# A graph-attention layer on one core: all q rows from gathered rows of h, and the ring of k|v rows used for the opening's loads

## The chip, the cores and the metric

The kernel runs on one core of one Trainium2 chip. The metric is device time in microseconds (us). Before the change the median of three runs is 1938.27 us (1937.52 to 1938.92). The profile shown here is of one execution with a span of 1932.2 us.

A core has five engines with queues of their own: TensorE (PE; PEld is its weight load), VectorE (DVE), ScalarE (ACT), GpSimd (POOL) and SyncE (SP, which only issues transfers here). Products of PE go to PSUM, in buffers that another engine has to read out before they are used again.

## The reference

There are 4096 nodes with 512 features. `adj` is a 4096x4096 matrix of 0 and 1, symmetric, with about 0.4% of ones and a full diagonal. One layer is computed:

```python
hs = layer_norm(x, ln1_scale, ln1_bias)            # sources
ht = layer_norm(h_target, ln1_scale, ln1_bias)     # targets
q = (ht @ Wq + bq).reshape(T, 8, 64) / 8
k = (hs @ Wk + bk).reshape(S, 8, 64)
v = (hs @ Wv + bv).reshape(S, 8, 64)
logits = where(adj != 0, einsum('thd,shd->hts', q, k), -1e30)
ctx = einsum('hts,shd->thd', softmax(logits), v)
ht = layer_norm(ht + ctx @ Wo + bo, ln2_scale, ln2_bias)
out = layernorm(x + ht + gelu(ht @ W1) @ W2)
```

W1 is 512x2048 and W2 is 2048x512. All numbers are float32.

## The kernel before

The kernel doesn't compute the dense logits. A target has some 17 neighbours on average, so it lists the neighbours of each target and gathers their k and v.

**k|v rows.** `project` takes x in 16 groups of 256 rows. `norm` loads a group, takes its moments and scales it; `turn` transposes it on PE and adds scale and bias on the way out of PSUM (L868); `source` multiplies it by Wk and Wv (L878), copies both products on ACT into one row of 1024 numbers (L880) and writes it to the table `kvd` in DRAM.

**Neighbour lists.** `edges` handles a tile of 128 targets. Its adjacency comes in four quarters of 128x1024, loaded into two buffers named `a` (L680). ACT takes the Sign of a quarter and counts its ones (L695), DVE numbers the ones and picks them with a maximum of eight (L699 to L725). `sort` orders the targets of one half (part A: the first 16 tiles, part B: the others) by their number of neighbours, and scatters their records (neighbour list, own index, moments of h) to DRAM, so that each sorted tile of 128 targets has a small cap on its list.

**q rows.** For the 16 tiles of part A, `front` gathers the rows of `h_target` that a sorted tile needs, scales them by the moments in the record, transposes them and multiplies them by Wq (L954 to L969). For part B, `target` computes q of all rows in their original order after the k|v rows (L889 to L900), writes q and the normalized row to a table `tqd`, and `front` only gathers from this table. In `finish` the normalized row is then added to the attention output, for part A with four transposes on PE into the same PSUM buffer (L1043), for part B with an add on DVE (L1056).

**Attention.** A ring of 17 slots of 128x1024 takes gathered k|v rows (L924, on POOL), one neighbour per slot, up to three slots at a time (`S`). DVE multiplies k by q (L1150) and sums by head (L1154), ACT takes Exp (L1158), DVE weights the v of two slots (L1103), ACT that of the third (L1123), and PE adds them up by transposing them into one PSUM buffer (L1111). For part B DVE first adds two slots (L1107). Gathers run four such steps ahead (`AHEAD`). A slot is free again when PE has read it. `finish` divides by the sums, multiplies by Wo (L1048) and applies the second layer norm.

**Feed-forward.** `feed` takes one group of two tiles (one tile for the first and the last group), multiplies by W1 (L1258), applies Gelu (L1261), multiplies by W2 (L1267), and `end` adds x, normalizes and scatters the rows to the output. W1 and W2 are loaded in four quarters by `load_quarter`.

**Order.** `_weave` merges several Python generators into one program by a running sum of costs that each yields; a planner may still move instructions within an engine's queue. Each engine then executes its queue in order. There are two weaves. The first holds `projections` (k|v rows, then part B's q rows), `prepare` (part A's lists and sort), `fill` (three more tiles of lists at double cost) and `begin` (the first three tiles of attention). The second holds attention, feed-forward, and the remaining lists with part B's sort.

Of the kernel before, what the change touches and what calls it, by code (L numbers as in the profile page):

```python
# [17 lines left out]
P = 128  # L18
# [425 lines left out]
def adj_resnorm_kernel(  # L444
# [66 lines left out]

    tqd = dram.tile([NBT * P, 2 * D], F32, name="tqd")
# [19 lines left out]
    with tc.tile_pool(name="keep", bufs=1) as keep:  # L532
# [17 lines left out]
        with ExitStack() as late:  # L550
# [5 lines left out]
            kvw = src.enter_context(tc.tile_pool(name="kvw", bufs=1))  # L556
            mid = ExitStack()
# [5 lines left out]
            first_x = ip.tile([P, G, D], F32, name="xin", bufs=3)  # L563
# [48 lines left out]
            def late_constants():  # L612
# [9 lines left out]
                                               ap=[[0, P], [1, D]]))  # L622
                pb = psi.tile([P, D], F32, name="pq", bufs=3)
# [49 lines left out]
            held, moms, hnorm = [], list(range(NT)), []  # L673
            mvh = wp.tile([P, NT, 2], F32, name="mvh")

            adjs = []

            def quarter(i, h):
                a = lp.tile([P, QW], I32, name="a", bufs=2)
                nc.sync.dma_start(a, adj[i * P:(i + 1) * P, h * QW:(h + 1) * QW])  # L680
                return a

            def edges(i):
# [4 lines left out]
                for h in range(NQ):  # L688
# [7 lines left out]
                    if n + 2 < NT * NQ:  # L696
                        adjs.append(quarter(*divmod(n + 2, NQ)))
# [59 lines left out]

            def moments(i):

                t = ip.tile([P, D], F32, name="hst", bufs=1)  # L760
                nc.sync.dma_start(t, h_target[i * P:(i + 1) * P, :])
                stats(ip, t, mvh[:, i, :], "n0")
# [60 lines left out]
            def project(order, t=None):  # L823


                state = {}

                def scaled(t, rs, nm):
                    nc.scalar.activation(t, t, AF.Identity, bias=nm, scale=rs)

                def norm(n, t=None):
                    if n >= len(order):
                        return
                    kind, g = order[n]
                    if t is None:
                        t = ip.tile([P, G, D], F32, name="xin", bufs=3)
                        nc.sync.dma_start(t, rows(x if kind == "x" else h_target, g))
                    if kind == "h":
                        rs, nm = hnorm[0]
                        for j in range(G):  # L840
                            i = g * G + j
                            scaled(t[:, j, :], rs[:, i:i + 1], nm[:, i:i + 1])
                        state[n] = t
                        return
                    mv = ip.tile([P, G, 2], F32, name="mv")
                    for j in range(G):
                        stats(ip, t[:, j, :], mv[:, j, :], "n1")
                    rs, nm = rstd_of(ip, mv, G, "n1")
                    for j in range(G):
                        scaled(t[:, j, :], rs[:, j:j + 1], nm[:, j:j + 1])  # L850
                    state[n] = t

                def turn(n):
# [3 lines left out]
                    bias = b1c if order[n][0] == "x" else b1r  # L857
                    hT = ip.tile([P, KC, GR], F32, name="hT")
                    for k2 in range(KC // 2):
# [6 lines left out]
                        for k in range(2):  # L866
                            kc = k2 * 2 + k
                            nc.scalar.activation(hT[:, kc, :], pt[:, k, :], AF.Identity,  # L868
                                                 bias=bias[:, kc:kc + 1], scale=s1c[:, kc:kc + 1])
                    state[n] = t, hT  # L870

                def source(n, j):
                    g, hT = order[n][1], state[n][1]
                    kvr = ip.tile([P, 2 * D], F32, name="row")
# [10 lines left out]
                def target(n, j):  # L885
                    g, hT = order[n][1], state[n][1]
                    pq = psi.tile([P, D], F32, name="pq", bufs=3)
                    for kc in range(KC):
                        nc.tensor.matmul(pq, hT[:, kc, j * P:(j + 1) * P], wq[:, kc, :],  # L889
                                         start=kc == 0, stop=kc == KC - 1)  # L890
                    pr = psi.tile([P, D], F32, name="pq", bufs=3)
                    for kc in range(KC):
                        nc.tensor.transpose(pr[:, kc * P:(kc + 1) * P],
                                            hT[:, kc, j * P:(j + 1) * P], ident)
                    tq = ip.tile([P, 2 * D], F32, name="row")
                    nc.vector.scalar_tensor_tensor(tq[:, :D], pq, HD ** -0.5, bqr,
                                                   op0=ALU.mult, op1=ALU.add)
                    nc.scalar.copy(tq[:, D:], pr)
                    r0 = (g * G + j - NA) * P
                    nc.sync.dma_start(tqd[r0:r0 + P, :], tq)  # L900
                    return 4.8

                with tc.manual_schedule(engines={mybir.EngineType.DVE}):
                    norm(0, t)
                    turn(0)
                    norm(1)
                yield 0.0
                for n, (kind, _) in enumerate(order):
                    while n + 2 < len(order) and order[n + 2][0] == "h" and not hnorm:
                        yield None  # L910
                    for j in range(G):
                        cost = (source if kind == "x" else target)(n, j)
                        if j == 0:
                            turn(n + 1)
                        else:
                            norm(n + 2)
# [24 lines left out]
            def front(i):  # L941
# [4 lines left out]
                if TILES[i][0] >= NA * P:  # L946
                    gather(tq, tqd, rec[:, ROW:ROW + 1])
                    tqs[i] = tq
                    return
# [27 lines left out]
            ring = kp.tile([P, RING, 2 * D], F32, name="kv")  # L977
# [31 lines left out]
            def finish(i, p, cps, group, hs, mv):  # L1009
# [3 lines left out]
                has = sp.tile([P, MAXE], BF16, name="has", bufs=1)  # L1013
                nc.vector.tensor_scalar(has[:, :cap], rec[:, E0:E0 + cap], 0.0, None, op0=ALU.is_gt)
                pm = sp.tile([P, MAXE, H], F32, name="pm", bufs=1)
                nc.vector.tensor_mul(pm[:, :cap, :], p[:, :cap, :],
                                     has[:, :cap].unsqueeze(2).to_broadcast([P, cap, H]))
# [21 lines left out]
                first = TILES[i][0] < NA * P  # L1039
                if first:  # L1040

                    for c in range(KC):
                        nc.tensor.matmul(pa[:, c * P:(c + 1) * P],  # L1043
                                         tq[:, D + c * P:D + (c + 1) * P], ident,
                                         is_transpose=True, start=c == 0, stop=False,
                                         skip_group_check=True)
                for c in range(KC):
                    nc.tensor.matmul(pa, ct[:, c, :], wo[:, c, :], start=c == 0 and not first,  # L1048
# [3 lines left out]
                if first:  # L1052
                    nc.scalar.copy(h, pa)
                    yield
                else:
                    nc.vector.tensor_add(h, pa, tq[:, D:])  # L1056
# [27 lines left out]

            def attention():
# [4 lines left out]
                def advance():  # L1090
                    for i in list(fronts):
                        step(fronts, i)
# [32 lines left out]
                for i in range(EARLY):  # L1125
                    prefetch(i)
                for i in range(EARLY):
                    fronts[i] = front(i)
# [303 lines left out]
```

## Time and profile before

| | PE | DVE | ACT | POOL |
|---|---|---|---|---|
| busy us | 1719.6 | 1443.7 | 1227.2 | 889.6 |
| share of the span | 89% | 75% | 64% | 46% |
| instructions | 7030 | 2637 | 3097 | 804 |

The transfers move 480 MB at a mean of 248 GB/s. Most of it is the gathers of k|v rows.

The page also cuts the span in 40 slices of 48 us. A digit is the busy share of a slice in tenths (9 is 90% or more); PEclk is the clock that was granted to TensorE in tenths of full speed, DMA the mean busy share of the 16 DMA engines:

```profile
PE   7978877788888889989999999899898989989996
...
DVE  5776764678797887757778789899897897878500
...
PEclk9989988889999899989999999999999999999998
DMA  9888867979878666567686888888878877776200
```

The first ten slices hold the opening (lists, k|v rows, part B's q rows, the first three tiles of attention), the last two or three the feed-forward that is left when attention is done. A busy digit of PE is not yet a rate: at a low clock the same work is busy for longer.

### The profile page before, as it was taken

How to read it: one execution, taken by the hardware profiler on the slowest of the kernel's cores; microseconds unless marked ns; L12 is line 12 of the kernel's file. 1: busy time of each engine (PE TensorE's matmuls, PEld its weight loads, DVE VectorE, ACT ScalarE, POOL GpSimd, SP SyncE). 2: the span in 40 equal slices, each digit the busy share in tenths (PEclk: the TensorE clock that was granted, in tenths of full speed). 3: DMA queues.
4: the chain of work that ended last, by engine and by line, in shares of the span. 5: the costliest groups of instructions: out<-in, count | busy, mean ns of one | idle time of the engine just before them, and what ended most of it. 6: DMA issues, size and time to landing. Idle time of an engine off the chain costs nothing. (4 is left out here: it accounts for less than half of the span.)

```text
span 1932.2 us, 23024 instructions
## 1 busy us (share of the span) xinstructions
PE 1719.6 (89%) x7030; PEld 1106.5 (57%) x7030; DVE 1443.7 (75%) x2637; ACT 1227.2 (64%) x3097; POOL 889.6 (46%) x804
## 2 busy tenths in 40 slices
PE   7978877788888889989999999899898989989996
PEld 3433333455566556657776666666565666656664
DVE  5776764678797887757778789899897897878500
ACT  5555654654786776657767677678686876666511
POOL 1000032524254445665575666777666655564201
PEclk9989988889999899989999999999999999999998
DMA  9888867979878666567686888888878877776200
GB/s 320 274 275 265 255 229 247 367 276 338 301 274 298 213 252 231 184 195 260 224 303 234 296 270 285 295 273 312 266 253 281 273 250 247 240 260 221 68 8 24
DMA packets 153262, 480.07 MB, mean 248 GB/s; under 512 B 24852, under 2 KB 29544, under 8 KB 153128
## 3 DMA queue, kind: packets, MB, share of 16 engines
q0 software_dynamic: 96720, 346.39, 52.3%
q1 hardware_dynamic: 48592, 109.03, 17.1%
q10 hardware_dynamic: 7816, 23.08, 3.0%
q8 instruction: 58, 0.95, 0.2%
q14 instruction: 76, 0.62, 0.1%
HBM read 439.15 MB, written 39.28 MB: 248 GB/s over the span
## 5 line engine op out<-in xcount | busy, mean ns | idle before, releaser
L924 POOL DMA_INDIRECT kv<-kvd,rec x603 | 697.4, 1157 | 495.1 <-PE cps L1111 201.0
L1267 PE MATMUL po<-w,gt 128*128 128x512 f32 x1024 | 476.2, 605 | 7.5 <-ACT gt L1261 4.0
L1258 PE MATMUL pf<-h2T,w 128*128 128x256 f32 (+1 forms) x2176 | 473.0, 370 | 5.3 <-DMA w<-in_L_gnn_W_dram 5.2
L1150 DVE TENSOR_TENSOR kv<-kv,tq 128x1536 f32<-128x1536 f32 (+2 forms) x211 | 352.2, 1676 | 135.5 <-DMA kv<-kvd,rec 108.5
L1258 PEld LDWEIGHTS pf<-h2T,w 128*128 128x128 f32 x2176 | 391.0, 192 | 75.3 <-issue 32.0
L1123 ACT ACTIVATE kv<-kv,pa 128x64 f32<-128x64 f32 x1520 | 390.4, 336 | 4.0
L1154 DVE TENSOR_REDUCE lg<-kv 128x24 f32<-128x1536 f32 (+2 forms) x211 | 350.2, 1666 | 1.6
L1267 PEld LDWEIGHTS po<-w,gt 128*128 128x128 f32 x1024 | 189.2, 195 | 192.8 <-issue 186.5
L1111 PEld LDWEIGHTS cps<-ident,kv 128*128 128x128 f32 x2008 | 237.8, 144 | 93.8 <-issue 47.2
L1111 PE MATMUL cps<-ident,kv 128*128 128x128 f32 x2008 | 263.1, 278 | 24.7 <-DVE kv L1107 17.5
L1103 DVE TENSOR_TENSOR kv<-kv,p 128x1024 f32<-128x1024 f32 (+1 forms) x211 | 249.5, 1188 | 25.7 <-ACT p L1158 24.4
L695 ACT ACTIVATE sg<-a 128x1024 uint8<-128x1024 int32 x128 | 135.0, 1056 | 161.1 <-DMA a<-in_adj_dram 126.0
L659 POOL TENSOR_TENSOR n_rs<-n_ve,mhalf 128x2 f32<-128x2 f32 (+2 forms) x51 | 46.9, 919 | 385.4 <-DVE n_ve L652 185.8
L878 PE MATMUL pq<-wv,hT 128*128 128x512 f32 x256 | 122.9, 624 | 20.1 <-ACT row L880 20.1
L1261 ACT ACTIVATE gt<-pf 128x512 f32<-128x512 f32 x128 | 76.4, 597 | 100.3 <-PE pf L1258 81.8
L878 PE MATMUL pq<-wk,hT 128*128 128x512 f32 x256 | 123.5, 625 | 17.0 <-ACT tq L954 10.5
L1261 ACT ACT_TABLE_LOAD x106 | 136.0, 1283 | 2.9 <-issue 1.2
L1048 PE MATMUL t<-wo,rb 128*128 128x512 f32 x256 | 126.3, 639 | 3.3 <-DVE rb L1035 3.3
L701 DVE MAX8 cand<-sg 128x8 uint16<-128x103 uint16 (+1 forms) x640 | 128.4, 251 | 0.7
L1158 ACT ACTIVATE p<-lg 128x24 f32<-128x24 f32 (+2 forms) x179 | 33.8, 189 | 130.5 <-DVE lg L1154 100.0
L878 PEld LDWEIGHTS pq<-wv,hT 128*128 128x128 f32 x256 | 50.0, 200 | 88.3 <-issue 57.0
L1158 ACT ACT_TABLE_LOAD x69 | 88.5, 1283 | 10.1 <-DVE lg L1154 9.0
(164 smaller groups left out, 1602.4 us busy)
## 6 DMA issues: line engine op xcount, KB each, us to landing
a<-in_adj_dram SPq DMA_DIRECT2D x128, 512.0 KB
kvd<-row ACTq DMA_DIRECT2D x32, 512.0 KB
kv<-kvd,rec POOLq DMA_INDIRECT x603
hst<-in_L_gnn_h_target_dram SPq DMA_DIRECT2D x32, 256.0 KB
tqd<-row SPq DMA_DIRECT2D x16, 512.0 KB
xin<-in_x_dram SPq DMA_DIRECT2D x15, 512.0 KB
rest_d<-gid SPq DMA_DIRECT2D x32, 160.0 KB
xin<-in_L_gnn_h_target_dram SPq DMA_DIRECT2D x8, 512.0 KB
```

Source lines behind the costliest of these rows:

```text
L695: nc.scalar.activation(sg, a, AF.Sign, accum_out=dpart[:, i, h:h + 1])
L701: nc.vector.max(cand[:, h * SQ + s, :], wd[:, w0:w1])
L878: nc.tensor.matmul(pkv, hT[:, kc, j * P:(j + 1) * P], w[:, kc, :], start=kc == 0, stop=kc == KC - 1)
L924: nc.gpsimd.indirect_dma_start(out=dst, out_offset=None, in_=table[:, :], in_offset=bass.IndirectOffsetOnAxis(ap=idx, axis=0))
L1103: nc.vector.tensor_tensor(v4, v4, p[:, j0:j0 + m, :].unsqueeze(3) .to_broadcast([P, m, H, HD]), ALU.mult)
L1111: nc.tensor.matmul(cps[:, c, :], kv[:, j, D + c * P:D + (c + 1) * P], ident, is_transpose=True, start=j0 + j == 0 and c == 0, stop=j0 + n ...
L1123: nc.scalar.mul(v, v, pa[:, hd:hd + 1])
L1150: nc.vector.tensor_tensor(kv[:, :n, :D], kv[:, :n, :D], tq[:, :D].unsqueeze(1).to_broadcast([P, n, D]), ALU.mult)
L1154: nc.vector.tensor_reduce(lg[:, :n, :], kv[:, :n, :D].rearrange("p j (h d) -> p j h d", h=H), AX.X, ALU.add)
L1258: nc.tensor.matmul(pf[:, k, :], w1[(f0 + k) // KC][:, kc, (f0 + k) % KC * P:((f0 + k) % KC + 1) * P], h2T[:, kc, :w], start=kc == 0, stop= ...
L1261: nc.scalar.activation(gt, pf, AF.Gelu_apprx_tanh)
L1267: nc.tensor.matmul(po[j], gt[:, k, j * P:(j + 1) * P], w2[(f0 + k) // KC][:, (f0 + k) % KC, :], start=False, stop=f0 + k == FC - 1, skip_g ...
```

## The change

The change does four things.

- All 32 sorted tiles get their q row from gathered rows of h in `front`. `target`, the table `tqd`, the second pass of h through `project` and the DVE add at the end of `finish` go.
- The ring of k|v slots exists from the start, and before the first gather its space takes the loads of the opening: 8 slots for adjacency quarters (`DEEP`), 4 slots for eight rows of h tiles, 5 slots for groups of x. So loads are asked for further ahead. `norm` is split in `request` (load, four groups ahead), `measure` (moments, three ahead) and `scale` (two ahead). The small buffers `hT` and `row` of the projection use the space of later buffers (`h2T`, `tq`).
- The first two quarters of W1 and W2 are loaded during the k|v rows, after the ninth and the eleventh group; the others at the start of the second weave. Wo and Wq are loaded later than before, at the fifth group.
- The weaves are set anew: the first holds the k|v rows, part A's lists, sort and first two fronts, and five more tiles of lists (`FILL`) at their plain cost. All of attention is in the second, and starts together with feed-forward.

Besides, the mask of filled list places in `finish` is fused with its multiplication into one instruction.

What it is for: to save the write and second read of part B's rows, to keep engines of the opening from waiting for transfers, and to let the opening be shorter.

```diff
+            ring = kp.tile([P, RING, 2 * D], F32, name="kv")
+            def xrows(n):
+                return ring[:, 12 + n % 5, :].rearrange("p (j d) -> p j d", j=G)
...
             def quarter(i, h):
-                a = lp.tile([P, QW], I32, name="a", bufs=2)
+                if i < NA + FILL:
+                    a = ring[:, (i * NQ + h) % DEEP, :].bitcast(I32)
+                else:
+                    a = lp.tile([P, QW], I32, name="a", bufs=2)
                 nc.sync.dma_start(a, adj[i * P:(i + 1) * P, h * QW:(h + 1) * QW])
...
-                    if n + 2 < NT * NQ:
-                        adjs.append(quarter(*divmod(n + 2, NQ)))
+                    ahead = min(n + DEEP - 1, n + 3 + n // 2)
+                    while len(adjs) < min(max(n + 3, min(ahead, (NA + FILL) * NQ)), NT * NQ):
+                        adjs.append(quarter(*divmod(len(adjs), NQ)))
...
+            def hrow(i):
+                return ring[:, DEEP + i // 2 % 4, i % 2 * D:(i % 2 + 1) * D]
             def moments(i):
-                t = ip.tile([P, D], F32, name="hst", bufs=1)
-                nc.sync.dma_start(t, h_target[i * P:(i + 1) * P, :])
+                while asked and len(asked) > NT - 4 - i:
+                    ask(asked.pop(0))
+                t = hrow(i)
...
-                tq = sp.tile([P, 2 * D], F32, name="tq", bufs=3)
-                if TILES[i][0] >= NA * P:
-                    gather(tq, tqd, rec[:, ROW:ROW + 1])
-                    tqs[i] = tq
-                    return
...
-                        cost = (source if kind == "x" else target)(n, j)
+                        cost = source(n, j)
                         if j == 0:
+                            request(n + 4)
+                            measure(n + 3)
                             turn(n + 1)
                         else:
-                            norm(n + 2)
+                            scale(n + 2)
...
-                if first:
-                    nc.scalar.copy(h, pa)
-                    yield
-                else:
-                    nc.vector.tensor_add(h, pa, tq[:, D:])
+                nc.scalar.copy(h, pa)
+                yield
...
-                for cost in _take(ed, 3 * steps):
-                    yield 2.0 * cost
+                for cost in _take(ed, FILL * steps):
+                    yield cost
...
-            _weave((projections(), 0), (prepare(), 0), (fill(), 0), (begin(), 0))
+            _weave((projections(), 0), (prepare(), 0), (fill(), 0))
...
-            t0 = UNIT / 2 * 3
-            _weave((att, t0 + PAUSE), (chain(feed(g) for g in range(len(GROUPS))), UNIT / 2 + LEAD),
-                   (other_lists(), t0 - 30.0))
+            _weave((att, 0), (chain(feed(g) for g in range(len(GROUPS))), 0), (other_lists(), WAIT),
+                   (weights(), 0))
```

## The prediction

> **What bounds the kernel now.** I read the table of stretches first, because the page's shares (PE 89%, DVE 75%) average four stages with different limits. The stages are cut where a line first or last appears: the k|v matmuls L878 end at 324 us, the feed-forward L1258 starts at 460, the last attention multiply L1150 is at 1801. Columns: stretch, its length, busy time and count of PE, PEld, DVE, ACT, POOL, then granted clock, DMA share, GB/s.
>
> ```profile
> 0.00:324.00 324.00, 264.11 (x680) 120.20 (x681) 218.82 (x903) 181.40 (x331) 42.59 (x58) 0.94 0.80 264
> 324.00:460.00 136.00, 108.46 (x401) 63.26 (x399) 91.42 (x189) 75.72 (x202) 46.25 (x43) 0.89 0.87 316
> ...
> 850.00:1000.00 150.00, 149.47 (x710) 106.11 (x709) 115.91 (x117) 106.59 (x296) 89.56 (x83) 1.00 0.77 260
> 1000.00:1815.00 815.00, 758.32 (x3291) 519.80 (x3290) 703.11 (x799) 581.49 (x1574) 512.41 (x440) 0.97 0.77 260
> ```
>
> From 850 to 1000 PE never pauses. From 1000 on PE (93%) and DVE (86%) hold each other: DVE waits for gathered rows, these for a free ring slot, the slot for PE. Before 460 nothing is full, so that is where time can be won. What stands there is in the waits of 0 to 324 us (engine, line, waited for: total us, times, longest):
>
> ```profile
> PEld pq L878 <- issue: 103.8, 404, 0.6
> ACT sg L695 <- DMA a<-in_adj_dram: 77.3, 42, 6.0
> DVE n_st L669 <- DMA hst<-in_L_gnn_h_target_dram: 32.0, 9, 6.4
> PEld pq L878 <- ACT row L880: 31.8, 20, 5.7
> ...
> PE pq L878 <- ACT row L880: 20.4, 11, 4.8
> ```
>
> ACT's Sign waits 77 us for adjacency, since only two quarters are in flight; the copy L880 that empties PSUM stands behind it, and PE waits 20 us for that copy. The timeline of DVE shows how attention opens (start, length):
>
> ```profile
> 348.07 1.76 DVE L1150 TENSOR_TENSOR kv<-kv,tq 128x1536 f32<-128x1536 f32 x1 [9.38 <-DMA kv<-kvd,rec]
> ```
>
> The first attention multiply is at 348, the first feed-forward matmul at 460. In these 112 us only 13 of 211 multiplies run.
>
> **The Trainium skill.** "DMA: Bandwidth & Descriptors", "Issuing engines are not separate DMA queues": transfers from SyncE, ScalarE and GpSimd interleave on the same 16 DMA engines. The trace agrees: with three issuers the rate is 264 GB/s at a share of 0.80, so a full share would be 264/0.80 = 330. "TensorE: Matmul & The Clock Gate", "Architectural detail: the array is 16× 32×32, not 1× 128×128": ACT and DVE are strict FIFO; hence the copy behind the Sign, as above. Same page, "Part 1: The HAM clock gate": the array falls back to half rate when idle and returns after sustained work. It fits: after a pause of 7.12 us at 352.8 four L893 transposes take 1.12 us, elsewhere 0.60. An idle opening costs twice.
>
> **The change, part by part.**
>
> *Loads in the opening.* Adjacency gets 8 ring slots in place of 2 buffers, x 5 in place of 3, h 4 rows of slots in place of 1. Nothing is computed less. The statistics of x run three groups ahead and Wo, Wq come later. I look for a new end of the opening as the largest of three floors.
> - PE: 8 records of 128x512 start 3.44 us apart (287.89 to 291.33), 0.43 each. A row tile has 16 of them, 6.9 us, and four transposes of 0.11 each: 7.3 us. 32 tiles take 234. With 7 for bias constants (8 matmuls of two records), 8 for two early q rows and the first start at 17: 266 us.
> - DVE: 219 us busy by 324, with 19 edge tiles scanned (154 Sign records at two each = 77 quarters). In the new order of instructions 23 tiles stand ahead of the first attention multiply. An edge tile is 9.8 us by its groups (L701 128, L699 52, L720 46, the rest 88, over 32), about 8.5 after overlap: 219 + 4 x 8.5 = 253, from a start near 19: 272.
> - DMA: 85.6 MB went by 324. Four adjacency tiles of 2.1 MB and two weight quarters (4.2 MB) are added, the early h reloads drop (about 1.5): 97 MB with the tiles loaded for the gap after it; some 90 before the last k|v row. At 330 GB/s: 273 us.
>
> Three streams near 270 us don't overlap perfectly; I take 90% of full for the fullest: about 300 us to the last k|v row. Bounds: 280 (97%) and 320 (nothing gained beyond the Wo/Wq reordering).
>
> *From there to attention.* Before, 24 us pass from the last L878 (324) to the first multiply (348), with 2 MB of weights loading at the same moment. After, these weights come earlier (at the 9th and 11th group); the last row still has to land and three gathers of about 1.2 us to be issued and land. I take 12 us: 312, a gain of 36. Bounds 292 and 332.
>
> *The 112 us to the first feed-forward matmul.* All 16 target groups' work goes: 128 L889 records (0.43), 64 L893 and 64 of the L864 transposes (0.11), 55 + 14 = 69 us of PE; also 8 h reloads, 16 writes and 16 gathers of 4 KB rows. In the new order attention has run 25 slots (about 9 multiplies) before the first feed-forward matmul, with one edge tile among it. Each takes 1.75 + 1.74 + 1.21 = 4.7 us on DVE, 5.2 with finish work: 47 + 10 for edges and waits = 57; I take 60. DVE sets this pace, PE has some 25 us to do and idles. Bounds 50 and 75. Gain 52. But two multiplies less are done by then than before (about 11): + 8 us.
>
> *q of the later 16 tiles on the way.* Each front gains four transposes, 8 records for q, and four transposes to add the row to the Wo result: 0.44 + 3.4 + 0.44 = 4.3 us of PE, 69 in all, in the stretch where PE is at 93%. ACT gains a scaling (0.81), four PSUM reads (0.46 each) and a copy (0.57), 3.2 us a tile, 51 in all; it is at 71% there. DVE exchanges the add L1056 (0.68) for the q scaling L969 (0.69). New waits: ACT's scaling waits for the h gather; the Exp and the third slot's products queue behind it, and DVE and PE for these. Before, the 16 early tiles waited so for 43.9 us in all, most at the first ones (14.5), so little is added: 0 to 15. PE ran at 100% while DVE was at 77%, so PE can fill more of the stretch than 93%: (758 + 69)/0.965 = 857 against 815, + 42. With little else I take 40. Bounds: 12 (PE at 100%) and 76 (PE stays at 93% and takes its share of throttle and waits: 69/0.93 + 2).
>
> *At nothing:* dropping the `has` mask (32 x 0.17 = 5.6 us of DVE) is hidden by PE's bound; the fewer gathered bytes (4.2 MB of tq rows, 13 us of DMA at 330) likewise, where the share is 0.77. Quarters 2 and 3 of the weights load while PE has no feed-forward to do, as before.
>
> Sum: 1938 - 36 - 52 + 8 + 40 = **1898 us**.
>
> **Rivals.**
> 1. *The openings reach their floors and PE takes q in its gaps*: first multiply 295 (- 53), 50 to the feed (- 62), + 8, + 20: **1851 us**. For it: 850 to 1000 at 100% PE, and DVE's load falls slightly. Against: 0.90 was the best DMA share held for 50 us in the opening, and PE is held by ACT, not by loads alone.
> 2. *The gain is spent by the idle opening of attention*: first multiply 325 (- 23), 72 to the feed (- 40), + 8, + 55: **1938 us**, no change. For it: nothing but 25 us of work for PE in that gap, at half rate.
> 3. *q is worth more where it was*: before, it ran on PE while DVE opened attention, so 69 us were half free; now they stand in the full stretch. With first multiply 330 (- 18), 75 to the feed (- 37), + 8, + 76 and 5 for ACT's wait on the gather: **1972 us**, slower. For it: PE at 93%, and DVE's 64 us of waits for rows after 1000, which a later PE lengthens. Against: DVE is no fuller than before.
>
> **From the cases to the numbers.** Mine 0.50, rival 1 0.26, rival 2 0.08, rival 3 0.16. Faster: 0.50 + 0.26 + 0.02 of rival 2 = 0.78; same 0.04; slower 0.02 + 0.16 = 0.18. Range: from rival 1's 1851 to above no change, 1945, leaving out the far halves of rivals 1 and 3, about 0.2.
>
> **What would show it.** Right: the wait of Sign for adjacency falls from 77 to under 30 us, L880 no longer holds PE, the last k|v matmul is near 300 and the first multiply near 312, the first feed-forward matmul near 372; PE has a hole of 30 us or more between; after 1000 PE is at 95% or more. Wrong in the first step: the DMA share rises to 0.95 and k|v still ends past 320. Wrong in the last: PE stays at 93% after the opening and the end moves by the full 69 us. If instead the distance from feed start to the end doesn't grow at all, rival 1 holds.

## The result, and the profile after

The changed kernel takes 1877.26 us (median of 4 runs, 1875.06 to 1880.62), the kernel before on the same chip 1937.89. The ratio is 0.9694, with a 95% interval of 0.967 to 0.9717: 61 us less. The time forecast was 1898 us, with a range of 1851 to 1945.

The profiled execution spans 1878.9 us (before 1932.2). Its slices, each now 47 us:

```profile
PE   7999784698998989999999989899999999999996
...
DVE  7999855989998837787878889888777778777400
...
PEclk9999987698999989999999999999999999999998
DMA  9999958888887657777778778777677767666000
```

The opening is full earlier (PE 7999, DVE 7999, DMA 9999), and the feed-forward starts nearly two slices sooner. In the seventh and eighth slice PE falls to 4 and 6, and its clock to 0.7 and 0.6: attention opens there, and PE waits for its first rows and then for DVE. A second dent is in the fifteenth slice (DVE 3).

The same in numbers, cut where a line ends or begins (stretch, length, busy time and count of PE, PEld, DVE, ACT, POOL, then granted clock, DMA share, GB/s). The last k|v matmul L906 ends near 294, the first feed-forward matmul L1266 starts at 372, the last attention multiply L1158 is at 1740:

```profile
0.00:294.00 294.00, 257.48 (x672) 119.47 (x673) 236.16 (x1006) 185.99 (x343) 41.79 (x57) 0.96 0.90 327
294.00:372.00 78.00, 37.93 (x148) 25.83 (x146) 63.16 (x98) 37.20 (x124) 47.88 (x40) 0.71 0.91 339
...
850.00:1000.00 150.00, 143.44 (x676) 99.63 (x675) 117.76 (x119) 106.24 (x293) 96.61 (x86) 0.99 0.78 265
1000.00:1740.00 740.00, 698.57 (x2984) 468.36 (x2983) 603.69 (x634) 538.30 (x1423) 430.59 (x379) 0.98 0.73 243
```

The opening is 30 us shorter with transfers at a share of 0.90 (0.80 before). PE idles for 40 of the 78 us from 294 to 372. After 1000, PE is at 698.57/740 = 94.4% (93% before), DVE at 82% (86% before).

The waits of the first 324 us, which answer to those of the kernel before (engine, line, waited for: total us, times, longest):

```profile
ACT sg L715 <- DMA kv<-in_adj_dram: 17.0, 9, 7.6
...
PEld pq L906 <- ACT tq L908: 16.4, 13, 6.5
...
ACT sg L715 <- DMA a<-in_adj_dram: 12.0, 4, 5.6
PE pq L906 <- ACT tq L908: 11.0, 4, 5.7
DVE n_st L684 <- DMA kv<-in_x_dram: 10.2, 8, 2.5
```

The Sign waits 29 us for adjacency (17.0 + 12.0) in place of 77. PE's wait for the copy that empties PSUM (L880 before, L908 now) is halved, 20.4 to 11.0 us, but not gone.

Four marks describe each kernel. All runs are in this table: time, and ratio to the kernel before as measured on the same chip in the same series; the marks are from the profiled execution, in us. "k|v" is the end of the last k|v matmul, "multiply" the first attention multiply, "feed" the first feed-forward matmul, and the last column goes from there to the end of the span.

| kernel | time | ratio (95%) | k\|v | multiply | feed | feed to end |
|---|---|---|---|---|---|---|
| before | 1937.9 | 1 | 324.6 | 348.1 | 460.7 | 1471.5 |
| after | 1877.3 | 0.9694 (0.967 to 0.9717) | 294.8 | 315.8 | 371.9 | 1507.0 |
| e1_shallow_adj | 1914.9 | 0.9882 (0.9855 to 0.9909) | 315.1 | 341.5 | 395.7 | 1520.8 |
| e9_shallow_both | 1916.3 | 0.9933 (0.9903 to 0.9962) | 307.4 | 336.5 | 391.6 | 1519.7 |
| e10_shallow_x | 1888.9 | 0.9769 (0.9732 to 0.9805) | 307.1 | 328.5 | 385.6 | 1505.8 |
| e2_late_w | 1883.3 | 0.9756 (0.9721 to 0.979) | 299.4 | 322.8 | 377.7 | 1503.7 |
| e5_q_alone | 1940.1 | 1.0021 (1.0007 to 1.0036) | 338.3 | 363.1 | 432.1 | 1507.4 |
| e11_loads_alone | 1916.5 | 0.9867 (0.9827 to 0.9907) | 304.1 | 322.4 | 464.9 | 1450.4 |
| e3_q_twice | 1926.0 | 0.9943 (0.9922 to 0.9964) | 296.1 | 317.0 | 373.2 | 1551.0 |
| e4_q_quarter | 1851.9 | 0.9573 (0.9548 to 0.9599) | 297.2 | 319.3 | 375.3 | 1475.8 |
| e8_spread_dep | 1873.8 | 0.9693 (0.9659 to 0.9726) | 295.5 | 317.5 | 373.9 | 1499.5 |
| e12_pair_all | 1847.9 | 0.9565 (0.9539 to 0.959) | 296.9 | 319.6 | 374.4 | 1473.9 |
| e13_pair_half | 1868.8 | 0.9676 (0.965 to 0.9702) | 294.0 | 314.3 | 370.3 | 1494.5 |
| e14_after_again | 1875.7 | 0.97 (0.9675 to 0.9725) | 295.7 | 316.3 | 372.4 | 1506.0 |

The change is read from the first two rows: the feed-forward starts 88.8 us earlier, and the rest takes 35.5 us longer. That is 53.3 us between the two profiled executions; the medians are 61 us apart, because the profiled execution before was shorter than its median (1933.9 us of device time against 1937.9) and the one after was longer (1880.6 against 1877.3). The last row is the changed kernel run again in the last series: it repeats within 2 us, and its marks within 1 us.

The series ran on different chips. The kernel before took 1937.9 us beside the changed kernel, 1936.1 beside e1, e3, e4 and e5, 1931.0 beside e2, e8, e9 and e10, 1942.3 beside e11, and 1933.9 beside e12, e13 and e14. So a difference of medians between two series can be off by some 10 us, and the ratios are given beside it where that matters. One of the 20 executions of e5_q_alone was in a slow state (2279.31 us at a granted clock of 0.742), and its ratio leaves it out.

### The profile page after: what moved, and what is told of

Its sections match the earlier page's. It is cut to its first block, busy times and chain, and to the rows that moved or that the text cites. A ratio compares the mean times of both kernels' runs of the same rounds, so it can differ in the third digit from the quotient of the medians.

```text
span 1878.9 us, 22938 instructions
## 1 busy us (share of the span) xinstructions
PE 1705.1 (91%) x7030; PEld 1100.5 (59%) x7030; DVE 1432.2 (76%) x2591; ACT 1247.5 (66%) x3139; POOL 885.2 (47%) x804
## 5 line engine op out<-in xcount | busy, mean ns | idle before, releaser
L941 POOL DMA_INDIRECT kv<-kvd,rec x603 | 684.1, 1134 | 492.2 <-PE cps L1129 217.2
L1266 PE MATMUL pf<-h2T,w 128*128 128x256 f32 (+1 forms) x2176 | 475.9, 371 | 3.4 <-issue 2.6
L1275 PE MATMUL po<-w,gt 128*128 128x512 f32 x1024 | 469.4, 600 | 0.0
L1158 DVE TENSOR_TENSOR kv<-kv,tq 128x1536 f32<-128x1536 f32 (+2 forms) x211 | 352.6, 1677 | 107.2 <-DMA kv<-kvd,rec 84.5
L1266 PEld LDWEIGHTS pf<-h2T,w 128*128 128x128 f32 x2176 | 391.0, 193 | 68.8 <-issue 23.4
L1129 PE MATMUL cps<-ident,kv 128*128 128x128 f32 x2008 | 269.8, 282 | 52.9 <-DMA kv<-kvd,rec 20.4
L674 POOL TENSOR_TENSOR n_rs<-n_ve,mhalf 128x2 f32<-128x2 f32 (+2 forms) x51 | 51.3, 1005 | 333.8 <-DVE n_ve L667 136.7
L980 PE MATMUL t<-wq,tq 128*128 128x512 f32 x256 | 119.9, 612 | 16.0 <-ACT tq L974 13.1
L906 PE MATMUL pq<-wk,h2T 128*128 128x512 f32 x256 | 124.0, 628 | 11.2 <-ACT h2T L896 5.8
L906 PE MATMUL pq<-wv,h2T 128*128 128x512 f32 x256 | 118.2, 604 | 6.0 <-ACT tq L908 5.9
L715 ACT ACTIVATE sg<-kv 128x1024 uint8<-128x1024 int32 x84 | 88.6, 1056 | 47.2 <-DVE cand L722 20.6
L1056 PE MATMUL t<-wo,rb 128*128 128x512 f32 x256 | 117.9, 604 | 1.5 <-DVE rb L1046 1.5
L906 PEld LDWEIGHTS pq<-wk,h2T 128*128 128x128 f32 x256 | 50.0, 202 | 78.2 <-issue 60.2
```

The source lines that it names most:

```text
L906: nc.tensor.matmul(pkv, hT[:, kc, j * P:(j + 1) * P], w[:, kc, :], start=kc == 0, stop=kc == KC - 1)
L941: nc.gpsimd.indirect_dma_start(out=dst, out_offset=None, in_=table[:, :], in_offset=bass.IndirectOffsetOnAxis(ap=idx, axis=0))
L980: nc.tensor.matmul(pq, hT[:, kc, :], wq[:, kc, :], start=kc == 0, stop=kc == KC - 1)
L1129: nc.tensor.matmul(cps[:, c, :], kv[:, j, D + c * P:D + (c + 1) * P], ident, is_transpose=True, start=j0 + j == 0 and c == 0, stop=j0 + n ...
L1158: nc.vector.tensor_tensor(kv[:, :n, :D], kv[:, :n, :D], tq[:, :D].unsqueeze(1).to_broadcast([P, n, D]), ALU.mult)
L1266: nc.tensor.matmul(pf[:, k, :], w1[(f0 + k) // KC][:, kc, (f0 + k) % KC * P:((f0 + k) % KC + 1) * P], h2T[:, kc, :w], start=kc == 0, stop= ...
```

## The experiments

The theory: the deeper loads bring the last k|v row forward; taking part B's q rows out of the opening of attention brings the feed-forward forward; and q is paid for, in part, in the second stretch. Its rivals: only one of the two halves does anything, or the weights loaded early do.

### The depth of the loads

e1_shallow_adj keeps two adjacency quarters in flight, as before:

```diff
-                    a = ring[:, (i * NQ + h) % DEEP, :].bitcast(I32)
+                    a = ring[:, (i * NQ + h) % 2, :].bitcast(I32)
...
-                    ahead = min(n + DEEP - 1, n + 3 + n // 2)
+                    ahead = n + 3
```

> The changed kernel with only two adjacency quarters in flight, as before the change; x, h, the weights and all else as changed. My theory (the opening got shorter because ACT's Sign no longer waits for adjacency and so no longer holds the copies behind it): Sign's waits for adjacency rise from 17 us to 60 to 80 us before the last k|v row, this row moves from 294 us to 315 to 325, and the end by as much: 1897 to 1910 us. Rival (x and h loads asked for further ahead, or Wo and Wq loaded later, made the difference): the last k|v row stays below 302 and the time below 1886.

It costs 38 us (1914.9 us; 36 by the ratios), and the wait that the theory names is back. Waits of its first 330 us:

```profile
ACT sg L715 <- DMA kv<-in_adj_dram: 96.1, 50, 5.9
...
DVE sg L720 <- ACT sg L715: 58.1, 30, 15.2
```

The last k|v matmul is 20 us later and the feed-forward 24. The remaining 14 us come after that (1520.8 against 1507.0). By the first feed-forward matmul only 92 adjacency quarters are scanned, where the changed kernel has 96, and 10 attention multiplies are done, where it has 12; that the debt of lists is what those 14 us pay is likely but wasn't isolated.

e10_shallow_x leaves adjacency deep and requests x only when it is measured, two groups ahead; e9_shallow_both does both.

```diff
                         if j == 0:
-                            request(n + 4)
-                            measure(n + 3)
                             turn(n + 1)
                         else:
+                            request(n + 2)
+                            measure(n + 2)
                             scale(n + 2)
```

> The changed kernel with deep adjacency loads, but the rows of x requested only when measured, two tiles ahead, as before. Theory A: with adjacency deep, the depth of x matters little, for rows of x are 8 MB of the opening's traffic and the scaling two tiles ahead leaves slack: last k|v row 295 to 301 us, total 1877 to 1885 us. Rival B: x bears a share as large as the adjacency's 20 us: last k|v row over 308 us, total over 1893 us.

> The changed kernel with both load depths of before: two adjacency quarters in flight, and the rows of x requested only when measured, two tiles ahead. Theory A: depth of loads made the whole gain of the opening, and x has a share of its own: last k|v row at 318 to 324 us (kernel before 324.0, two adjacency quarters alone 314.5), total 1918 to 1928 us. Rival B: the adjacency is the only load whose depth counted: last k|v row within 3 us of 314.5, total within 4 us of 1915.

x alone costs 12 us (ratio 0.9769), its k|v rows end 12 us late: more than the theory allowed, less than the rival. With both shallow the k|v rows end at 307, earlier than with adjacency alone (315), which neither theory had; in this mark, of one execution each, the two depths don't add. In the total that is undecided: by the medians both cost 39 us and adjacency alone 38, but by the ratios both cost 2.4% of the time of before, adjacency 1.9% and x 0.75%, and the first two have intervals that touch.

Depth isn't all of the opening's gain, either. With both depths as before, the k|v rows still end 17 us earlier than in the kernel before (307.4 against 324.6). The rest of the change in the opening (deeper loads of h, Wo and Wq later, the new order) must bring these, and no run takes it apart.

### The weights

e2_late_w asks for all quarters of W1 and W2 behind the k|v rows in the program. The planner moves one of them forward: in the trace one quarter is issued at 118 and 155 us and three between 273 and 303, where the changed kernel issues two at 151 to 187 and two at 267 to 300. So the run delays one early quarter.

```diff
-                    if n in (8, 10):
-                        load_quarter(wp2, n // 2 - 4)
...
-                    yield 10.0
-                    load_quarter(pool, q + 2, nc.scalar)
+                    yield 5.0
+                    load_quarter(pool, q, nc.scalar)
```

> The changed kernel without the early load of W1 and W2: quarters 0, 1 and 2 are requested when attention opens, and the planner puts quarter 3 near the end of the opening. Theory A: the opening carries 2 MB less, 6 us at the 327 GB/s of the changed kernel's opening, and the stretch to the first feed-forward matmul, which ran at 339 GB/s with 0.91 of the transfer engines busy, 4 MB more, 12 us: first feed-forward matmul 4 to 10 us later than 371.9, total 1880 to 1888 us. Rival B: transfers do not set either stretch, total within 3 us of 1877.

1883.3 us, 6 more (12 by the ratios); the feed-forward starts 5.9 us later. Theory A holds in size by the medians and by the mark. The delay of one quarter is the smallest effect measured here, though its ratio's interval overlaps that of e10_shallow_x.

### The q rows, moved alone and kept

e5_q_alone is the kernel before with one part of the change: part B's q rows come from gathered rows of h, as in the changed kernel.

```diff
-                if TILES[i][0] >= NA * P:
-                    gather(tq, tqd, rec[:, ROW:ROW + 1])
-                    tqs[i] = tq
-                    return
...
-            order = xs + hs[NA // G:]
+            order = xs
```

> The kernel before with one part of the change alone: part B's q rows from gathered rows of h (the target pass, its table and the DVE add go); loads, weights and the order of the weaves stay. My theory (two gains that add up): the last k|v row stays at 320 to 328, the first attention multiply near 345, the first feed-forward matmul moves from 460 to 400 to 415, from there to the end some 35 us more as in the changed kernel: 1908 to 1925 us, a third to a half of the gain. Rival A (the q part is the whole gain): below 1890. Rival B (without the loads it brings nothing, because the q work in the opening was hidden beside attention's opening): 1932 or more.

It gains nothing: 1940.1 us, ratio 1.0021. From the first multiply to the feed-forward pass 69 us in place of 113, and the stretch behind grows by 35.9 us (35.5 in the changed kernel): that would be 8 us won. But the feed-forward starts only 28.6 us earlier, since the k|v rows end 14 us later. The planner put two fronts of part A ahead of the last row tiles. Timeline of ACT (start, length, work, idle time before it and what ended that):

```profile
306.70 0.81 ACT L950 ACTIVATE tq<-tq,rec 128x512 f32<-128x512 f32 x1 [14.15 <-DMA tq<-in_L_gnn_h_target_dram,rec]
```

and of PE:

```profile
308.50 5.48 PE L878 MATMUL pq<-wk,hT 128*128 128x512 f32 x8 [10.34 <-ACT hT L868]
```

ACT stood 14 us for a gather of h, and the copies of the k|v rows stood behind it. So this run gives a price of q in the second stretch, but it isn't a clean reading of what the opening gains.

e11_loads_alone turns this around. It is e2_late_w with part B's q rows put back behind the k|v rows (`target`, the table `tqd` and its gathers); beyond that the two programs differ only in buffers that this needs (a k|v row has buffers of its own again) and in the tile's last add, on DVE as before.

```diff
-            order = list(range(NG))
+            order = [("x", g) for g in range(NG)] + [("h", g) for g in range(NA // G, NG)]
...
+                if TILES[i][0] >= NA * P:
+                    gather(tq, tqd, rec[:, ROW:ROW + 1])
+                    tqs[i] = tq
+                    return
```

> The deep loads of the changed kernel without its other half: the q rows of part B's sixteen tiles are made from rows of h in order and written to a table, behind the last k|v rows as in the kernel before, and gathered from there (W1 and W2 are loaded late, as in e2_late_w, for room; all work is kept). Theory A: with the q rows gone from the second stretch, feed to end falls by the 36 us that e5_q_alone showed, to 1465 to 1475 us, and the opening of attention, where PE stood idle for 40 of 78 us in the changed kernel, takes 69 us of q at a price of 25 to 50 us: first k|v multiply 315 to 330 us, first feed-forward matmul 400 to 425 us, total 1868 to 1895 us; then moving q is worth within 1% of nothing with deep loads too. Rival B: q fills the idle PE of that opening, first feed-forward matmul before 395 us: total 1840 to 1865 us, faster than the changed kernel, so that moving q cost time. Rival C: the q rows, 12 MB more of loads and stores in a stretch whose transfer engines were at 0.91, hold the gathers and the feed start as long as before, past 440 us: total over 1900 us, and moving q is worth over 1.5% once the loads are deep.

1916.5 us against 1883.3: 33 us by the medians, but 21 us (1.1% of the time of before) by the ratios, since the two ran on different chips. The multiply starts at the same time in both (322). From there to the feed-forward pass 142 us with q there and 55 without; after it, 1450 and 1504 (not all of it q: 115 adjacency quarters are scanned before the later start, 95 before the earlier). Rival C has the total and the late start right; its 1.5% isn't shown, and its reason is only half of what happens. Stretches of e11_loads_alone, columns as above:

```profile
300.00:372.00 72.00, 59.26 (x188) 30.47 (x186) 42.67 (x77) 40.88 (x109) 16.50 (x17) 0.89 0.82 317
372.00:410.00 38.00, 32.10 (x150) 19.62 (x148) 31.87 (x131) 20.07 (x40) 7.43 (x8) 1.00 0.83 272
410.00:450.00 40.00, 13.69 (x54) 8.89 (x55) 22.90 (x36) 10.61 (x34) 14.08 (x14) 0.62 1.04 404
```

PE works through q until 399 us, and the transfer engines are not full there (0.82, 0.83). GpSimd has stopped gathering, and the waits of 300 to 465 us say for whom:

```profile
POOL kv L967 <- PE cps L1163: 82.3, 3, 64.4
POOL kv L967 <- DMA kvd<-row: 35.3, 1, 35.3
...
PE t L1001 <- ACT rb L1074: 29.3, 1, 29.3
ACT rb L1074 <- issue: 23.3, 1, 23.3
```

The ring is full, and a slot is only free when PE has summed its v rows (L1163). That work stands behind all q matmuls in PE's queue, so one wait lasts 64.4 us. In the kernel before, attention was woven among the q matmuls, and the same wait came in smaller pieces (its waits of 324 to 460 us):

```profile
POOL kv L924 <- PE cps L1111: 55.3, 8, 13.2
```

A second stop follows that isn't q's own work: from 406 us PE waits 29.3 us for a copy on ACT (L1074), and ACT stands 23.3 us before that copy. In its queue six issues of weight loads stand in a run, from 412.95 to 434.89 us; the first three take 0.4 to 0.6 us each, the others 7.65, 7.32 and 5.35 us. Timeline of ACT:

```profile
414.51 7.65 ACTq L574 DMA_DIRECT2D w<-in_L_gnn_W_dram  x1
422.18 7.32 ACTq L573 DMA_DIRECT2D w<-in_L_gnn_W_dram  x1
429.54 5.35 ACTq L574 DMA_DIRECT2D w<-in_L_gnn_W_dram  x1
434.93 0.59 ACT L1074 COPY rb<-t 128x512 f32<-128x512 f32 x1 [23.33 <-issue]
```

e2_late_w has all its weight loads issued by 303 us, at 0.4 to 0.6 us each. So the difference of the two runs holds a stall of 22 us in which no q is worked on, and an order of q that is harsher than that of the kernel before. It doesn't price the move of q. What it shows is the wait of 64.4 us: rival B's idle PE was there, but filling it in that order stopped the gathers.

### What a matmul costs in the second stretch

e3_q_twice does part B's q matmuls twice, the first time for nothing: 55 us more for PE. e4_q_quarter does a quarter of them, 41 us less, and leaves three quarters of q's sum out.

```diff
-                for kc in range(KC):
-                    nc.tensor.matmul(pq, hT[:, kc, :], wq[:, kc, :], start=kc == 0,
-                                     stop=kc == KC - 1)
+                for _ in range(2 if i >= NA else 1):
+                    for kc in range(KC):
+                        nc.tensor.matmul(pq, hT[:, kc, :], wq[:, kc, :], start=kc == 0,
+                                         stop=kc == KC - 1)
```

```diff
-                for kc in range(KC):
+                kcs = KC if i < NA else 1
+                for kc in range(kcs):
```

> The changed kernel with the four Wq matmuls of every part B tile done twice into the same PSUM buffer (the second pass starts anew): 16 x 8 more records of 0.43 us = 55 us of PE work in the full stretch, nothing else. My theory (PE holds that stretch, with a part of such work hidden in its pauses, as 35 of 69 us of q showed): 25 to 45 us slower, 1902 to 1922. Rival A (PE's pauses take it, DVE holds the stretch): under 15 us. Rival B (every us of PE work there is a us of time): 55 us or more, 1932 and up.

> The changed kernel with one instead of four Wq matmuls for every part B tile: three quarters of q's sum are left out there, so the attention weights of these tiles are not the reference's. 16 x 6 records of 0.43 us = 41 us of PE work less in the full stretch. My theory (PE holds it in part): 15 to 30 us faster, 1847 to 1862. Rival A (DVE and the gathers hold it): under 8 us. Rival B (PE alone): 41 us, 1836.

The doubled q costs 49 us, 0.88 of what it adds; the quarter saves 25, 0.62 of what it takes away. The stretch from 1000 to 1740 us of the first:

```profile
1000.00:1740.00 740.00, 703.90 (x2944) 462.66 (x2943) 577.00 (x603) 509.37 (x1359) 410.74 (x365) 0.99 0.70 232
```

and of the second:

```profile
1000.00:1740.00 740.00, 691.72 (x3034) 471.64 (x3033) 618.42 (x692) 558.93 (x1469) 448.84 (x382) 0.98 0.73 244
```

With more q, PE rises to 95.1% and DVE falls to 78%; with less, PE is at 93.5% and DVE at 84%. By the time from feed to end, which leaves out what the opening varies by, the two prices are 44.0/55 = 0.80 and 31.2/41 = 0.76. The quarter falls within the theory's range. The added q falls outside all three: a us of PE costs here some 0.6 to 0.9 of its length, more than the theory's share and less than rival B's whole.

### A hole that costs little

In the changed kernel sixteen record scatters of part B stand in one run in GpSimd's queue, and the gathers behind them come late; this is the dent of the fifteenth slice. e8_spread_dep makes the index of each scatter depend on an attention step:

```diff
+                nc.vector.scalar_tensor_tensor(ranki[:, i:i + 1], lg[:, 0, 0:1], 0.0,
+                                               rank[:, i:i + 1], op0=ALU.mult, op1=ALU.add)
```

> The changed kernel, with the sixteen record scatters of part B no longer issued in one run on GpSimd's queue: each scatter's index is made with one small DVE operation that also reads the logits of an attention step, so that one goes out per step, between the gathers of k|v rows. All work is kept, and 16 operations of one element a lane are added. In the changed kernel the stretch 676 to 692 us had PE at 9.8 of 16 us while DVE waited for gathered k|v rows behind the scatters. Theory A: this hole sits on the path that sets the end, so taking it away brings 8 to 15 us: 1862 to 1870 us, PE near full in 650 to 700. Rival B: the hole is paid anyway by a later backlog, or the scatters cost each gather as much when spread: within 4 us of the changed kernel's 1877.

Theory A's 8 to 15 us don't come: ratio 0.9693, as the changed kernel's 0.9694, and 3.5 us less by the medians, which is rival B's range. Stretches of e8_spread_dep:

```profile
600.00:700.00 100.00, 91.08 (x404) 62.22 (x404) 72.89 (x93) 66.56 (x172) 51.67 (x50) 0.97 0.58 193
700.00:850.00 150.00, 143.66 (x657) 98.55 (x656) 111.48 (x122) 101.54 (x279) 91.55 (x82) 0.99 0.68 228
```

and of the changed kernel:

```profile
600.00:700.00 100.00, 85.64 (x343) 55.08 (x344) 62.12 (x81) 55.15 (x142) 54.10 (x53) 0.90 0.53 167
700.00:850.00 150.00, 149.98 (x703) 104.67 (x702) 118.17 (x118) 111.00 (x300) 85.08 (x76) 1.00 0.72 241
```

The hole is gone, 5.4 us of PE's work come earlier, and the next 150 us give 6.3 back. PE was held up in the changed kernel but had a backlog to make good with, and did so at 100%. A rest can't be excluded: from the feed-forward's start to the end the profile of e8_spread_dep is 7 us shorter (1499.5 against 1507.0 and 1506.0), with one execution of it.

### Taking work off PE

These runs say that PE's length counts, in part, from 316 us to the end, and that DVE has room. In part B, DVE already adds two of three value rows before PE sums them. e12_pair_all does this in part A too, e13_pair_half in every other step of it:

```diff
-                    if m > 1 and i >= NA:
+                    if m > 1:
```

```diff
-                    if m > 1 and i >= NA:
+                    if m > 1 and (i >= NA or j0 // S % 2):
```

> The changed kernel with one more use of VectorE: in part A too, the first two value rows of each step of three are added on DVE (0.685 us, as in part B) before PE transposes and sums them, which takes 4 records of 0.123 us off PE. About 100 steps: PE 49 us less and DVE 68 us more between 316 and 1050 us. All work is kept. Theory A: PE's path set the stretch that took q (each us of PE taken off brought 0.6 in e4_q_quarter), and DVE at 0.81 to 0.83 there has room: 15 to 30 us less than the changed kernel, 1847 to 1862 us. Rival B: DVE, which would be at 0.92, becomes the bound of part A, and gathers wait for slots of k|v rows that it frees late: within 6 us of the changed kernel or slower.

> As e12_pair_all, but in part A only every other step adds the pair on DVE: PE 24 us less, DVE 34 us more between 316 and 1050 us. All work is kept. Theory A: 8 to 15 us less than the changed kernel, 1862 to 1869 us, half of what e12_pair_all brings. Rival B: the two engines are in balance at this point, so this one beats e12_pair_all. Rival C: no change beyond 4 us, since what PE gains in part A is waited for elsewhere, as with the spread scatters of e8_spread_dep.

> The changed kernel once more, unedited, on the chip of e12_pair_all and e13_pair_half, so that differences of half a per cent between versions of it can be read: 1872 to 1881 us, 0.967 to 0.972 of the kernel before.

e12_pair_all takes 1847.9 us, 28 less than the changed kernel on the same chip (1875.7): the fastest version that does all the work. Stretches of it:

```profile
700.00:850.00 150.00, 141.91 (x607) 95.03 (x608) 132.17 (x142) 110.32 (x299) 93.42 (x84) 0.97 0.78 262
850.00:1000.00 150.00, 141.31 (x603) 94.45 (x602) 135.38 (x146) 113.19 (x313) 103.87 (x89) 0.98 0.81 271
```

DVE rises from 79% to 88 and 90% there, and loading it so far still paid; PE's busy time over the span falls by 48 us (1705.1 to 1657.1), of which 28 arrive. e13_pair_half takes 22 us off PE (1705.1 to 1682.6), but its median is only 6.9 us below the changed kernel's (1865.6 to 1872.2 us against 1869.5 to 1880.1), and the intervals of the two ratios overlap: a small gain is likely, but not clear. Rival B fell, since all pairs beat half of them; why half bring so much less than half stays open.

## Why the prediction was right, step by step

**Last k|v row, "about 300": 294.8.** The three floors were 266 to 273 us, and 90% of full was taken for the fullest. The transfers did run at a share of 0.90, and e1_shallow_adj shows that adjacency's wait is a cause: with it the wait is 96 us, without it 29, and the rows end 20 us apart. The sizes below the 300 were off in both directions. The transfers moved 96 MB by then (327 GB/s for 294 us), not 90; their full rate, taken as 330 GB/s, comes out as 327/0.90 = 363 here; and DVE was busy for 236 us, not 253. So the hit within 5 us is in part luck, and which of the three floors holds the opening wasn't tested.

**First multiply at 312: 315.8.** The stretch from the last row was taken as 12 us and took 21. Timeline of ACT in the changed kernel:

```profile
296.01 0.58 ACT L908 COPY tq<-pq 128x512 f32<-128x512 f32 x1 [3.48 <-DMA kvd<-tq]
...
298.91 0.60 ACT L908 COPY tq<-pq 128x512 f32<-128x512 f32 x1
299.55 0.33 ACTq L910 DMA_DIRECT2D kvd<-tq  x1
```

The rows of k|v now share the three `tq` buffers with the fronts, which hold two of them: the last copy waits 3.48 us for its own predecessor's write. Its write is issued at 299.55, the first gather starts at 305.85, and the multiply follows 10 us later. The term had the write's landing and three gathers in it, but they alone took 16 us, and it left this buffer out. The two errors in the opening, 5 us early and 9 late, cancel in part.

**60 us to the feed-forward, start near 372: 56 us, 371.9.** The reasoning "DVE sets this pace" stands: of the 56 us DVE is busy for 54 and PE for 30. That the feed-forward starts at 372 to the us is luck: 4 us late at the multiply, 4 us early from there. All versions of the changed kernel with q moved, loads deep or shallow, need 54 to 57 us for it. e5_q_alone needs 69, and e11_loads_alone, with q and the stalled ACT there, 142. The hole of PE is there, and costs clock as foreseen. Timeline of PE:

```profile
302.54 3.70 PE L980 MATMUL t<-wq,tq 128*128 128x512 f32 x8 [0.78 <-DVE tq L982]
326.67 2.82 PE L1129 MATMUL cps<-ident,kv 128*128 128x128 f32 x12 [20.42 <-DMA kv<-kvd,rec]
...
903.63 1.47 PE L1129 MATMUL cps<-ident,kv 128*128 128x128 f32 x12
```

After 20 us of waiting, twelve records (instructions in the trace) take 2.82 us where they take 1.47 at full clock.

**"Two multiplies less are done", + 8.** Only one less was done (12 against 13): twelve came where nine were expected, and the working put the kernel before at 11, though its own reading above had 13. The two slips nearly offset each other.

**q on PE's path, + 40.** Together with those 8 us, 48 were expected and 35.5 came. This is the term that was mis-sized. It let PE rise from 93% to 96.5% over the stretch; after 1000 us PE got only to 94.4%, so the forecast "95% or more" fell too. Yet the stretch ended sooner: the working sized it from PE's share after 1000 us alone. The 35.5 us aren't one thing, either. 26.9 of them lie between the first feed-forward matmul and the last attention multiply. The other 8.6 come after that multiply (139.4 us to the end, 130.8 before), where q is done; the working has no term for them, and why they came is open. In e5_q_alone, where the edit is q alone, the parts are 31.3 and 4.6 us. So that run prices the move of q at half of its length (35.9/69 = 0.52), and at less if what comes after the last multiply isn't q's. "All of PE's time counts" isn't true either: e3_q_twice and e4_q_quarter, around the changed kernel, give 0.76 to 0.80 from feed to end. Why the 69 us were cheaper than the next 55 was not separated.

**The sum.** Forecast −40 us, of it −88 for the start of the feed-forward and +48 after. Measured in the profiles −88.8 and +35.5; the rest of the difference to the medians' −61 is between executions. The forecast was 21 us too long in the medians. By the ratios, 2.4 of the 3.1% gained go with the depth of the loads (e9_shallow_both takes them back). What the move of q gains by itself, with deep loads and in the order of before, no run prices.

**The rivals.** The first (1851) was right that the second stretch takes q for well under its length, wrong that the multiply comes at 295. The second needed the opening's gain to be lost, and the feed-forward started 88.8 us earlier. The third needed q to be dearer where it went than where it was. Two runs lean against that, and neither is clean. In e5_q_alone the stretch from multiply to feed-forward is 43.6 us shorter and what follows 35.9 longer. In e11_loads_alone the feed-forward starts 87 us later, up to 22 of it from ACT's stall, and what follows is 53 us shorter. The third rival's picture of q as half free in the opening missed that q stood ahead of work that frees ring slots: 55.3 us of GpSimd's waits before.

## What to carry to other kernels

Buffers that stand empty until a later stage are a place for deeper loads in an earlier one; but look for all streams that are short, for one short stream (adjacency) alone took back more than half of the 61 us. Filling an idle engine is no gain if the filling stands, in its queue, ahead of the work that frees a buffer for the transfers: in e11_loads_alone q held the gathers for 64 us in one wait. Issues of loads in the queue of an engine that also computes can do the same: six of them held ACT for 22 us there. So a contrast of two programs has to be read in its trace before its difference is given to the edit. And a hole in the busiest engine need not be worth much (e8_spread_dep: 5.4 us of PE, most of it made good later), while work put on that engine or taken off it moved the end by three to nine tenths of its length; e12_pair_all, which moves some of it to an engine at 79%, beat both kernels.

## What the runs showed of the hardware

The full rate of the transfer engines isn't one number. A share of 0.80 at 264 GB/s gave an estimate of 330 GB/s; the changed kernel's opening had 0.90 at 327 (363), and 410 to 450 us of e11_loads_alone, where gathers, weights and adjacency came together, 1.04 at 404 (388). A share above 1 says that the share itself is rough. What sets the rate was not isolated; the three stretches differ in their mix of loads, stores and gathers.

PE was slower after a pause, seen twice: twelve transposing records in 2.82 us after 20 us of waiting (1.47 us at 903 us), and in e5_q_alone eight of 128x512 in 5.48 us after 10.34 us, where the next eight took 3.60.

An issue of a load can hold its engine: of six issues of 1 MB in a run on ACT's queue, three took 0.4 to 0.6 us and three 5.35 to 7.65 (e11_loads_alone). What the long ones waited for the profile doesn't show.
